# Two transformer layers on one core: router logits computed transposed, slot counts made by products, and the join of the layers filled with more shared-expert tiles

## The chip, the cores and the metric

The kernel runs on one core of one Trainium2 chip. A core has a matrix engine (TensorE, PE in the profile, its weight loads PEld), a vector engine (VectorE, DVE), an activation engine (ScalarE, ACT), a general engine (GpSimd, POOL) and a queue that only issues transfers (SyncE, SP). Each engine takes its instructions strictly in the order in which the program lists them for it; an instruction that waits holds up everything behind it on the same engine. The metric is the device time of one launch in microseconds (us); lower is better.

## The reference

Activations x have the shape 4 batches x 512 tokens x 256 features, all in float32. Two layers are applied, each with a modulated layer norm before an attention part and before a feed-forward part:

```python
h = layernorm(x) * (1 + ca) + sa;  x = x + ga * attention(h)
h = layernorm(x) * (1 + cb) + sb;  x = x + gb * ffn(h)
```

The six modulation vectors of a layer come from `silu(c) @ wmod`. In layer 0 the attention is linear (one key-value sum per feature), and the feed-forward part is a mixture of experts: a router with 32 experts in 8 groups (the best 3 groups are kept, softmax, best 6 experts), at most 48 token slots per expert over all batches, filled in the order of the tokens, so that they fill up early; and two shared experts for every token:

```python
logits = x @ gate_w.T                      # tokens x 32
pos  = cumsum(one_hot(flat_e)) - 1         # place of a pair in its expert
buf  = zeros(E * C + 1, h).at[slot].set(x[tok_idx])
out  = sum_k topk_w * expert(buf)[slot] + silu(x @ ws_g) * (x @ ws_u) @ ws_down
```

In layer 1 the attention is causal softmax attention (16 heads of 128), and the feed-forward part is a gated one whose three weights are made by cubic interpolation from control points.

## The kernel before

The work is staged in time like this; the stages overlap only at their edges.

**Front (0 to 148 us).** Modulation vectors, layer norm, linear attention, second norm and routing of the four batches. `choose(b)` (L546) makes the router logits: for each of the four 128-token tiles and each half of the features, a product with the 128x128 block of normalized activations as stationary operand and the 32 columns of the router weights as moving operand (L551). Each such product stands in the trace as two matmul records. Then some thirty small DVE instructions pick groups and experts; the 0/1 choices of a batch are `selb`, and a running sum of all earlier choices, `carry`, is made on DVE (L613, L615). `place(b)` (L617) turns choices into slot numbers by products on PE: a triangular matrix times `selb`, `ones` times the `carry` (L624), and `ones` times the earlier tiles of the batch (L628); then DVE compares the slot numbers with all the 48 slots (`oh`, L659), PE counts tokens from that (`pix`, L663). The shared experts' first products (`shared`, L706, tiles `sg` and `su`) have no one waiting for them and fill PE.

**Experts (148 to 230 us).** Sixteen pairs of experts. The order of PE is written out by hand in the loop at L960; the other engines' order is made by a planner that follows an estimate of each instruction's cost, except where `tc.issue_after(ins)` puts a block's instructions behind `ins` on that instruction's engine. For a pair q: the rows are fetched by an indirect transfer (`fetched`, `xg`, 8 buffers), turned (`turned`), multiplied with the pair's weights (`gate_up`), activated (ACT L822, DVE L823), turned again (`act_turned`), multiplied down (`down`), scaled into `ysb` (ACT L851, 4 buffers for the first 12 pairs) and written to two tables in memory, `ytab` by SP (L882) and `planes` by POOL's scatter (L867). Weights lie in 8 slots and are loaded as slots come free. Sixteen tiles of the shared experts' second product (`shared_down`, L724, tile `pd`, evicted by ACT at L735) are spread over the stage: four ahead of the loop, one in each of the iterations 0 to 5 (L967), two and four after the loop (L992, L994, L1002). The weights of layer 1's first three heads are loaded behind the last expert weights (L974), and ACT multiplies the three query weights by a constant (`scale_q`, L770, called at L1010).

**Join (about 216 to 245 us).** The twelve scattered pairs are read back from `planes` (`yr`, L921, 4 x 768 KB), summed and gated on DVE and POOL (`gated`, L932), the last four pairs are added through products (`combined`, `pcs`, `add_transposed`), which finishes x of batch 0. Then `norm(0)` of layer 1: statistics on DVE (L192, L193), a power on POOL (L196), normalization on DVE and ACT (L208, L212), eight turns on PE (L226, tile `lt_a`), eviction by ACT (L228) and DVE (L232), and the first projections (`project_first`).

**Heads (245 to 985 us) and feed-forward of layer 1 (985 to 1164 us).** 64 batch-head units. PE's order is written by hand (L1519 on). Between them run, on DVE, ACT and POOL, the interpolation of the weights (`spline`), the combination of its parts (`ffn_forms`, POOL, L1061) after units 1, 4 and 7, the gathers of expert results for batches 1 to 3 (POOL, L281), and the norm of the next batch. `ffn_norm(0)` is called at head 59 (L1586) for the first feed-forward batch.

## Time and profile before

| | us |
|---|---|
| three timed runs | 1163.98, 1165.59, 1167.76 (median 1165.59) |
| the profiled execution | 1165.69, span of its instructions 1164.0 |
| PE busy (share of the span) | 1118.4 (96%) |
| DVE, POOL, ACT busy | 850.9, 621.0, 541.5 |
| front, until the first `pd` product | 148.3 |
| experts, from there to the end of the last shared tile | 148.3 to 235.4 |
| turns of norm(0) of layer 1 | from 238.4 |

The profile gives each engine's busy time, the groups of instructions by source line, who waited for whom, and a timeline. In a row of the timeline the first number is the start in us from the first instruction, the second the length of the merged run, then engine, line, operation, written and read tiles, shapes, and in square brackets the idle time of that engine before the row and what ended it. PE and PEld rows overlap. A busy PE is not one at its peak: a matmul's record is longer than the time it takes from the next. The clock column says what share of its clock PE was granted in a stretch.

### The profile page before, as it was taken

The page shows a single profiled execution, that of the slowest core. Times are in us where ns is not written, and L with a number is a line of the kernel's source. Part 1 is how long each engine was busy: PE and PEld are TensorE (multiplying, and loading weights), DVE is VectorE, ACT ScalarE, POOL GpSimd, SP SyncE. Part 2 cuts the span into 40 slices and gives each one's busy share as a digit, 9 for nine tenths or more (in the row PEclk, how much of TensorE's full clock was granted, in tenths as well). Part 3 has the DMA queues.
Part 4 walks back from the last instruction along what each step waited for, and adds up shares of the span by engine and source line. Part 5 has one row for each costly group of instructions (what it writes and reads, how often), then busy time and mean ns, then how long its engine had stood idle before and what let it go on. Part 6 is the DMA issues. An engine that isn't in the chain of part 4 may idle for free.

```text
span 1164.0 us, 16910 instructions
## 1 busy us (share of the span) xinstructions
PE 1118.4 (96%) x5231; PEld 822.6 (71%) x5231; DVE 850.9 (73%) x2573; ACT 541.5 (47%) x1380; POOL 621.0 (53%) x944
## 2 busy tenths in 40 slices
PE   7888999989999999999999999999999999999998
PEld 2444364557777777777777777777787777888887
DVE  5687534567878887888887887988877777566765
ACT  3652223345555555555555465555555455333321
POOL 4363224248874857864656975444635655344331
PEclk9998999899999999999999999999999999999999
DMA  7921379734411322520321431012010000000001
GB/s 264 289 68 46 98 238 287 223 101 95 77 46 53 67 68 38 91 68 28 78 40 43 95 64 60 28 37 69 19 46 19 25 13 1 1 1 19 19 1 36
DMA packets 80485, 86.09 MB, mean 74 GB/s; under 512 B 12158, under 2 KB 64748, under 8 KB 80268
## 3 DMA queue, kind: packets, MB, share of 16 engines
q1 hardware_dynamic: 67868, 70.19, 19.3%
q0 software_dynamic: 11712, 13.25, 7.2%
q10 hardware_dynamic: 816, 1.58, 0.4%
q8 instruction: 42, 0.69, 0.2%
q14 instruction: 47, 0.39, 0.1%
HBM read 73.84 MB, written 11.55 MB: 73 GB/s over the span
## 4 chain that ended last, share of the span: by engine, by line
PE 72%; DVE 8%; POOL 4%; ACT 3%; issue 2%; DMA 2%; SPq 0%; ACTq 0%; POOLq 0%; DVEq 0%
PE s L1308 10%; PE o L1349 10%; PE po L1044 7%; PE P0p L1044 6%; PE fP L1044 6%; PE pt L1340 5%; PE P1p L1044 4%; PE P2p L1044 4%; PE acc L1044 3%; PE P0v L1044 3%; PE P2v L1044 2%; PE P1v L1044 2%; POOL ysum L281 1%; PE gu L814 1%; PE sg L713 1%
## 5 line engine op out<-in xcount | busy, mean ns | idle before, releaser
L1323 ACT ACTIVATE p<-s,nm 128x512 f32<-128x512 f32 (+3 forms) x256 | 135.4, 529 | 117.2 <-DVE nm L1320 114.7
L1308 PE MATMUL s<-qk,qk 128*128 128x512 f32 (+3 forms) x512 | 170.1, 434 | 1.1 <-DVE qk L1216 1.0
L1349 PE MATMUL o<-pT,v 128*128 128x512 f32 (+3 forms) x512 | 148.8, 433 | 0.3 <-DVE u3v L1228 0.3
L1349 PEld LDWEIGHTS o<-pT,v 128*128 128x128 f32 x512 | 96.8, 190 | 55.4 <-issue 30.6
L1342 ACT COPY pT<-pt 128x512 f32<-128x512 f32 (+1 forms) x192 | 98.5, 513 | 68.2 <-PE pt L1340 66.5
L1320 DVE TENSOR_REDUCE nm<-s 128x1 f32<-128x512 f32 (+3 forms) x256 | 124.0, 484 | 4.0
L281 POOL DMA_INDIRECT ysum<-ytab,code x72 | 113.6, 1578 | 20.4 <-issue 15.2
L1325 DVE TENSOR_SCALAR p<-p,den 128x512 f32<-128x512 f32 (+3 forms) x256 | 116.9, 457 | 3.4
L1340 PEld LDWEIGHTS pt<-ident,p 128*128 128x128 f32 x640 | 81.6, 141 | 34.5 <-issue 10.5
L1340 PE MATMUL pt<-ident,p 128*128 128x128 f32 x640 | 101.7, 273 | 0.3 <-DVE p L1325 0.3
L1318 DVE TENSOR_TENSOR s<-s,mask 128x128 f32<-128x128 f32 x256 | 73.5, 287 | 32.3 <-PE s L1308 32.3
L1183 POOL TENSOR_TENSOR w_p<-w_q,w_k 128x128 f32<-128x128 f32 x63 | 38.9, 617 | 84.3 <-ACT t1p L1222 51.9
L1308 PEld LDWEIGHTS s<-qk,qk 128*128 128x128 f32 x512 | 77.5, 191 | 5.5 <-issue 1.1
L1044 PE MATMUL P0p<-hT_a,w_q 128*128 128x256 f32 x252 | 75.0, 379 | 0.0
L1191 POOL TENSOR_TENSOR w_p<-w_k 128x128 f32<-128x128 f32 x63 | 29.9, 475 | 81.3 <-PE P2p L1044 81.3
L1044 PEld LDWEIGHTS P0p<-hT_a,w_q 128*128 128x128 f32 x252 | 47.5, 190 | 33.1 <-issue 29.9
L1324 DVE RECIPROCAL den<-den 128x1 f32<-128x1 f32 x256 | 40.4, 158 | 38.5 <-ACT p L1323 34.4
L1044 PE MATMUL P1p<-fT,w_p 128*128 128x256 f32 x252 | 65.0, 380 | 2.4 <-POOL w_p L1185 1.3
L1360 ACT ACTIVATE oH<-o,bia 128x512 f32<-128x512 f32 x64 | 44.0, 687 | 42.7 <-PE o L1349 41.5
L1216 DVE SCALAR_TENSOR_TENSOR qk<-P0p,bia,u3p 128x256 f32<-128x256 f32 x63 | 30.4, 482 | 37.4 <-ACT qk L1237 36.2
L1052 POOL TENSOR_TENSOR fI<-it 128x256 f32<-128x256 f32 x30 | 21.8, 728 | 67.0 <-DVE it L1641 67.0
L1044 PEld LDWEIGHTS P1p<-fT,w_p 128*128 128x128 f32 x252 | 47.6, 190 | 10.1 <-issue 2.2
(336 smaller groups left out, 2676.9 us busy)
## 6 DMA issues: line engine op xcount, KB each, us to landing
wg<-in_w_gate_up SPq DMA_DIRECT2D x16, 704.0 KB
w_q<-in_w_q SPq DMA_DIRECT2D x64, 128.0 KB
w_k<-in_w_k SPq DMA_DIRECT2D x64, 128.0 KB
w_v<-in_w_v SPq DMA_DIRECT2D x16, 512.0 KB
wd<-in_w_down SPq DMA_DIRECT2D x16, 352.0 KB
basis<-in_basis SPq DMA_DIRECT2D x8, 640.0 KB
planes<-zero SPq DMA_DIRECT2D x4, 768.0 KB
yr<-planes SPq DMA_DIRECT2D x4, 768.0 KB
```

What stands on the lines that cost most here:

```text
L281: ga = nc.gpsimd.indirect_dma_start(out=ysum[b][:, i, :], out_offset=None, in_=ytab[:, :], in_offset=bass.IndirectOffsetOnAxis(ap=code[:, ...
L1044: nc.tensor.matmul(out, lhsT=lhsT, rhs=rhs, start=start, stop=stop, skip_group_check=shared)
L1308: nc.tensor.matmul(s[:, at[i] : c], lhsT=qk[n, 0][:, i * P : (i + 1) * P], rhs=qk[n, 1][:, : (i + 1) * P], start=True, stop=True,)
L1318: nc.vector.tensor_tensor(s[:, e - P : e], s[:, e - P : e], mask, ALU.add)
L1320: nc.vector.tensor_reduce(nm, s[:, e - w : e], AX.X, ALU.max, negate=True)
L1323: nc.scalar.activation(p, s[:, e - w : e], AF.Exp, bias=nm, accum_out=den)
L1324: nc.vector.reciprocal(den, den)
L1325: nc.vector.tensor_scalar_mul(p, p, den)
L1340: nc.tensor.transpose(pt[:, c : c + P], probs[n, i][:, j * P : (j + 1) * P], ident)
L1342: nc.scalar.copy(pT, pt[:, :w])
L1349: nc.tensor.matmul(o[:, j * P :], lhsT=vs[n // 4][:, j, hc : hc + HD], rhs=pTs[n, j], start=(j == 0), stop=(j == NTT - 1),)
L1360: nc.scalar.activation(oT, o, AF.Identity, bias=bia[:, 2, h : h + 1])
```

## The change

Four things change.

1. **Router.** The logits are made transposed: the 32 router columns are the stationary operand, 128 tokens the moving one, and the four token tiles go to four 32-column groups, so that one 128x128 tile `pl` comes out. ACT copies it to memory on the chip (`lgT`), and PE turns it into the former layout. `carry` is gone; `place(b)` multiplies `ones` with every tile of every earlier batch instead (4, 8 and 12 products for batches 1 to 3), for which `selb` has four buffers.
2. **Shared tiles.** The iterations 3 to 5 of the loop lose their shared tile. After the loop there are two, then six, then, behind the eight turns of norm(0), one more.
3. **Join.** norm(0) is called inside the expert stage, with its tile in a freed weight slot, and PSUM buffers of that stage; the turned activations lie in a pool that is open earlier. The three `scale_q` stand behind the eviction of the first of the six tiles. `xg` has 7 buffers and is fetched 7 pairs ahead.
4. **Heads.** The first three `ffn_forms` are called at heads 8, 15 and 24 (so far 8, 14 and 20) and stand behind a named POOL instruction; the statistics of `ffn_norm(0)` stand behind the last DVE eviction of head 59's projection.

```diff
+NTAIL = 7
-        return pool.tile([P, 2, T], F32, tag="hT", name=f"hT_{name}{b}")
+        return pool.tile([P, 2, T], F32, tag="hT", name=f"hT_{name}{b}", bufs=B if name[1] == "0" else 2)
...
+        class Freed:
+            def tile(self, shape, dtype, tag, name, bufs=None):
+                return freed(self.tag, self.pair, shape, name)
...
-            lgv = ps.tile([P, NTT, E], F32, tag="tr", name=f"plg{b}")
-            for i in range(NTT):
-                for k in range(2):
+            pl = ps.tile([P, P], F32, tag="tr", name=f"plg{b}")
+            for k in range(2):
+                for i in range(NTT):
                     nc.tensor.matmul(
-                        lgv[:, i, :],
-                        lhsT=hTs[b][:, k, i * P : (i + 1) * P],
-                        rhs=gwT[:, k, :],
+                        pl[32 * i : 32 * i + 32, :],
+                        lhsT=gwT[:, k, :],
+                        rhs=hTs[b][:, k, i * P : (i + 1) * P],
                         start=(k == 0),
                         stop=(k == 1),
                     )
+            lgT = rp.tile([P, P], F32, tag="lgT", name=f"lgT{b}", bufs=1)
+            nc.scalar.copy(lgT, pl)
+            lgv = ps.tile([P, NTT, E], F32, tag="tr", name=f"plv{b}")
+            nc.tensor.transpose(lgv.rearrange("p i e -> p (i e)"), lgT, ident)
...
-            if b + 1 < B:
-                c = carry[b + 1] = rp.tile([P, 1, E], BF16, tag="carry", name=f"carry{b}")
-                parts = [selb[:, i, :] for i in range(NTT)] + ([carry[b][:, 0, :]] if b else [])
-                nc.vector.tensor_tensor(c[:, 0, :], parts[0], parts[1], ALU.add)
-                for x in parts[2:]:
-                    nc.vector.tensor_tensor(c[:, 0, :], c[:, 0, :], x, ALU.add)
...
-            if b:
-                nc.tensor.matmul(
-                    pos, lhsT=ones, rhs=carry[b].to_broadcast([P, NTT, E]), start=False, stop=False
-                )
+            for c in range(b):
+                for i in range(NTT):
+                    nc.tensor.matmul(
+                        pos,
+                        lhsT=ones,
+                        rhs=chosen[c][0][:, i : i + 1, :].to_broadcast([P, NTT, E]),
+                        start=False,
+                        stop=False,
+                    )
...
-                if q + 8 < NPAIR:
-                    fetched(q + 8)
+                if q + 7 < NPAIR:
+                    fetched(q + 7)
...
-                    if q < NI - NEXP - 6:
+                    if q < NI - NEXP - NTAIL - 2:
                         shared_down(NEXP + q)
...
-                shared_down(NI - 6)
+                shared_down(NI - NTAIL - 2)
                 combined(NPAIR - 1)
-                shared_down(NI - 5)
+                shared_down(NI - NTAIL - 1)
...
-                for i in range(NI - 4, NI):
-                    last_down = shared_down(i)
+                for i in range(NI - NTAIL, NI - 1):
+                    pd_copy = shared_down(i)
+                    if i == NI - NTAIL:
+                        with tc.issue_after(pd_copy.ins):
+                            for n in range(3):
+                                scale_q(n)
+                    if i == NI - 3:
+                        before_norm = pd_copy
+                hTs1[0] = new_hT(w4, 0, "a1")
+                ln_transposed(
+                    Freed("wg", NPAIR - NLOAD + NTT), ps, "gu", 1, 0, SA, CA, hTs1[0], "a1", None, None, before_norm
+                )
+                with tc.issue_after(last_pow[0].ins):
+                    shared_down(NI - 1)
...
-        for n in range(3):
-            scale_q(n)
...
-        ffn_h[b] = new_hT(hp, b, "f1"), normalized(np_, b, "f1", None, after, after)
+        ffn_h[b] = new_hT(w4s[0], b, "f1"), normalized(np_, b, "f1", None, after, after)
...
+        EARLY_FORMS = (8, 15, 24)
...
-                if unit in (1, 4, 7):
-                    ffn_forms(unit // 3, early[:, unit // 3])
...
+            if n in EARLY_FORMS:
+                with tc.issue_after(last_form[0].ins):
+                    ffn_forms(EARLY_FORMS.index(n), early[:, EARLY_FORMS.index(n)])
...
-                ffn_norm(0)
+                ffn_norm(0, evicted[n])
```

## The prediction

> **What bounds the kernel now.** I read the busy shares first, then PE's waits, then the timeline around each wait, and last the stretches with their granted clock. The page says that PE is the bound; so a change is worth what it does to PE's idle time, to its slowed stretches, and to its work where it never waits.

> ```profile
> PE 1118.4 (96%) x5231; PEld 822.6 (71%) x5231; DVE 850.9 (73%) x2573; ACT 541.5 (47%) x1380; POOL 621.0 (53%) x944
> PE 72%; DVE 8%; POOL 4%; ACT 3%; issue 2%; DMA 2%; SPq 0%; ACTq 0%; POOLq 0%; DVEq 0%
> ```

> The wait table of PE names four places that the change touches:

> ```profile
> PE gu L814 <- DVE xT L807: 4.1, 1, 4.1
> PE lt_a L226 <- ACT xn_a L208: 3.0, 1, 3.0
> PE pix L663 <- DVE oh L659: 3.5, 2, 2.0
> PE P1p L1044 <- POOL w_p L1185: 1.3, 1, 1.3
> ```

> The first looks like a wait for DVE; the timeline follows it back. ACT stands in `scale_q(0)`, which waits 5.22 us for layer 1's query weights; behind it stands the activation of pair 12, behind that DVE, behind that PE:

> ```profile
> 204.85 0.42 ACT L770 ACTIVATE w_q<-w_q 128x256 f32<-128x256 f32 x1 [5.22 <-DMA w_q<-in_w_q]
> 205.29 0.32 ACT L822 ACTIVATE act<-gu 128x176 f32<-128x176 f32 x1
> 205.64 0.34 DVE L823 TENSOR_TENSOR act<-act,gu 128x176 f32<-128x176 f32 x1 [4.53 <-ACT act L822]
> 206.37 2.61 PE L814 MATMUL gu<-wg,xT 128*64 128x352 f32 x8 [4.07 <-DVE xT L807]
> ...
> 211.42 1.35 PE L814 MATMUL gu<-wg,xT 128*64 128x352 f32 x8
> ...
> 212.86 1.02 POOL L867 DMA_INDIRECT planes<-ysb,didx  x1 [4.19 <-ACT ysb L851]
> ...
> 216.77 2.06 SPq L921 DMA_DIRECT2D yr<-planes  x4
> ...
> 223.14 0.96 DVE L937 TENSOR_TENSOR yr<-yr 128x768 f32<-128x768 f32 x1 [3.10 <-DMA yr<-planes]
> ...
> 235.88 1.05 POOL L196 TENSOR_TENSOR rs_a<-rs_a,nhalf 128x4 f32<-128x4 f32 x1 [8.59 <-DVE rs_a L195]
> ...
> 238.40 2.13 PE L226 MATMUL lt_a<-ident,xn_a 128*128 128x128 f32 x8 [2.96 <-ACT xn_a L208]
> ```

> The first `gu` after the gap takes 2.61 us where the next takes 1.35: the rows by stretch show why. Their last three figures are the clock granted to PE, the DMA share and GB/s; the clock is 0.73, 0.74 and 0.72 here and 1.00 in the stretches beside them.

> ```profile
> 202.00:207.00 5.00, 0.93 (x6) 0.45 (x7) 1.28 (x8) 1.57 (x5) 0.28 (x1) 0.73 0.69 219
> 207.00:215.00 8.00, 8.00 (x46) 3.92 (x44) 4.03 (x20) 2.92 (x8) 2.31 (x4) 0.74 0.41 73
> 236.00:242.00 6.00, 3.59 (x10) 2.24 (x11) 3.35 (x6) 1.87 (x3) 5.43 (x9) 0.72 0.32 115
> ```

> The reader sees a chain: last scatter 212.86, read-back 216.77, DVE without a pause from 223.14 to 235.8, PE's turns 238.40. PE is ahead of it by 2.96 us, so what counts for the join is when the last scatter leaves.

> **Expert stage.** (a) `scale_q` moves behind the first of six shared tiles. Gone are 4.07 us of gap and the slow iteration: `gu` to `gu` is 5.05 us (206.37 to 211.42) against 2.83 for the next (to 214.25), so 2.22; sum 6.29. Moved past: ACT alone. There the three (1.26 us) now precede the copies of the later shared tiles; two PSUM buffers cover it, and if not, 1.26. (b) Three shared tiles leave iterations 3 to 5: 4.12 us per iteration (167.13 to 171.25) falls to 2.84 (179.50 to 182.34), 3 x 1.28 = 3.84. Together the loop could be 10.1 us earlier. (c) What is late next: the four `ysb` buffers. `ysb` of pair 11 needs the `ytab` write of pair 7 landed; that was issued at 191.55 and landed at 204.45 (landing events), and the DMA share is 0.87 to 1.05 from 150 to 202, so fewer PE instructions don't bring it forward. Pair 11's `ysb` stood at 211.64; without this limit it would be at 201.5, with it at about 204.5: I take 204.5, since DMA is full: 7.1 earlier, 10.1 as the bound. (d) Then the scatter 1.22 later (211.64 to 212.86) and its landing: 3.73 us for this one, 6.16 for the one at 198.41 with weights in flight; at 205.7 the last of them still land (208.2), so 4.9, and 0.2 to the read-back: 210.8 against 216.77, **6.0 earlier**. (e) `xg` with 7 buffers: a fetch leaves in iteration q+1 and is needed in q+5, 4 x 2.84 = 11.4 us less some 3.3 for `ysb`, scatter and issue; landings took 7.0 to 7.3. Nothing, with a margin of 0.8; if gone, up to 0.5 per pair on eight pairs, of which the limit in (c) hides 3. (f) PE before the turns: earlier by 7.9 (pair 12's `y` starts at 205.45 instead of 213.33), plus two tiles of 1.29 (24 matmuls in 5.36): 235.43 becomes 230.1, still ahead of the turns at 232.4, so those two cost nothing; if the loop were not earlier they would cost what exceeds 2.96. (g) The last tile behind the turns: 1.29, between turns that end at 240.5 and a second half of `hT` that DVE delivers at 241.43; the first products lay in there. Between 0.4 and 1.3, I take 0.9, because those products fill the hole already. (h) `w_o` and `basis` on SP may start some 10 us later, behind the freed slots; `w_o` landed at 237.0 and is first read at 276.9, `basis` at 239.4 and 308.6. Nothing. Sum: -6.0 + 0.9 = **-5.1** (bounds -9.2 with neither limit of (c) nor (d), -1 if `ytab` lands 2 later and a scatter takes 6.2 plus a wait in (e)).

> **Front.** Here the planner makes a new order, so this is the least certain part. Rows:

> ```profile
> 87.57 1.34 DVE L615 TENSOR_TENSOR carry<-carry,selb 128x32 bf16<-128x32 bf16 x2
> ...
> 90.95 0.35 PE L663 MATMUL pix<-oh,tok 128*32 128x384 bf16 x4 [1.97 <-DVE oh L659]
> ...
> 112.69 1.64 PE L551 MATMUL plg<-gwT,hT_m 128*128 128x32 f32 x14
> ...
> 101.39 0.59 ACT L721 ACTIVATE sT<-sg 96x512 f32<-96x512 f32 x1 [12.14 <-PE sg L713]
> ```

> Logits: 16 matmul records a batch at 0.106 us (1.48 between first and last of 14) are 1.7. The new ones stream 128 float columns, 0.107 each by the eight turns `at_d` (1.04 with 0.2 of latency): 1.7 if they go one by one, 0.4 if four column groups overlap as `pix` does (four of 384 columns in 0.35, eight in 0.51, so 0.16 for four). `pix` is the nearest; with the turn 0.25, a batch saves 1.0, bounds +0.3 and -1.1. Only where PE doesn't wait does it count: batch 3 whole (PE has 3.6 us of gaps between 108 and 148), the others by a third: -2.0. Counts: 24 products for 3, at 0.055 (starts of `pos`), 21 x 0.055 = 1.2, of it 0.6 in batch 3, and 0.3 of the rest: +0.9. DVE loses eleven adds, 3.4 us; in batch 1 they take 2.3 (0.69, 1.34, 0.28) just ahead of `posb` and `oh`, on which PE waits 1.97: -2.0. ACT copy and turn add 0.8 of latency a batch (0.37 as in L735, 0.27, two hand-overs). At the end that is covered: rows of pair 0 landed at 138.4 and are turned at 150.67. But PE stands at the turn if the planner leaves nothing in between; 0 to 3.2, and behind a waiting ACT up to 12.1 (last row). I take 1.0. `selb` with four buffers, `lgT` and the moved `hT` add no instruction: nothing. Sum **-2.1**, bounds -6.5 (the stretch at half clock from 91.7 to 98.5, 0.66 over 90 to 100, goes too, 3.4, with the further -1.0 of the copy) and +13.

> The trace has 32-column products among 128-column ones at `pix`: the next `sg` starts at 128.36, before the records of `pix` end (128.08 and 0.35), so no pause shows. [...]

> **Heads.** POOL's `ffn_forms(2)` at 495.3 stands behind four gathers and ahead of the weight forms for which PE waits 1.27 (the P1p row above); at head 24 no gathers stand: -1.27. `ffn_norm(0)` was run by DVE at 764.7 to 767.9, and PE waited 1.86 for a value eviction behind it (769.23); it moves to head 59, where DVE is busy 15.9 of 25: -1.86. There its chain (statistics 2.2, power 1.05, normalization 1.4) has one unit of 10.7 us before PE's turns: 0, or up to 3 if DVE puts it last; I add 0.6. The forms at heads 8 and 15 stay where POOL has no queue: nothing, or the 1.1 that POOL stood idle before those of 415.8. Sum **-2.5**, bounds -3.1 and +2.

> **Sum.** -5.1 - 2.1 - 2.5 = -9.7. The profiled execution took 1165.69 (span 1164.0, 1.7 around it), 0.1 above the median 1165.59: **1156.0**.

> The rows show 0.74 after the gap of 4.07 and 0.72 after that of 2.96, so the sum leaves the join's slowed products as they are behind its remaining gap of 2.3. [...]

> **Rivals.** *R1, the front gives its gain back*: copy and turn cost 1.8 a batch, 7.1, not 1.0: 1156 + 6.1 = 1162.1. For it: two PSUM buffers `tr` are now held at once by a batch's logits, and the next batch's turns use them. Against: PE has shared products in reserve until 148. *R2, transfers keep the expert stage where it is* (bounds of (c), (d), (e)): -1 instead of -5.1, 1160. For it: the DMA shares; against: expert weights land 11.7 us or more before use (pair 15's at 202.55, read at 214.25). *R3, slower*: at PE's new turn of `lgT`, TensorE stands in order behind ACT. One batch behind the 12.1 wait, with a half-clock stretch (3.4) after it, so 15.5 for the 1.0 in the sum: 1156 + 14.5 = 1170.5. It decides once the four turns together cost over 14.1 (1169.1 less 1156, and the 1.0). For: ACT idles 12.14 and 5.82 us behind `sg` in batches 2 and 3. Against: the copy needs only `pl`, which in batch 2 would be ready ahead of that `sg`. *R4, more*: no half-clock stretch at 92 (3.4), DMA no limit (4.1): 1148.5.

> **How the numbers follow.** 0.3% (3.5 us) is about what a measurement of this kernel can tell from no change: 1162.1 and 1169.1 are the lines. Chances: forecast 0.50 (own range 1152 to 1160), R1 0.16, R2 0.13, R3 0.13, R4 0.08. Faster: 0.50 + 0.13 + 0.08 + half of R1 0.08 = 0.79; same: the other half and a little of R3, 0.10; slower 0.11. The range leaves out R3 and the far half of R4, 0.17: 1149.5 to 1166.

> **What will show it.** Right: no ACT wait for `w_q` in the loop; read-back near 209 (front included); the first `gu` of pair 13 at about 1.35; turns of norm(0) near 230; no `plg` row over 0.6; no PE wait of over 1 us at 498 and 767. Wrong: PE idle before the turn of `lgT`; `ysb` waiting for `ytab` past 206; DVE late for head 59's `lt_f`. A new order by the planner in stages that the change doesn't touch would move the time without any of this.

## The result

The changed kernel took 1154.18 us in the median of six runs (1152.02 to 1155.01), the kernel before 1165.72 beside it: a ratio of 0.9894, 95% interval 0.9873 to 0.9915, or 11.5 us less. The forecast was 1156.0. The profiled execution took 1152.55, 1.6 below its median; its span is 1150.7 against 1164.0, so the two traces differ by 13.3, 1.8 more than the medians.

Two lines of the changed kernel's page, busy time and the chain that ended last by engine:

```profile
PE 1112.7 (97%) x5256; PEld 816.5 (71%) x5256; DVE 848.0 (74%) x2562; ACT 541.2 (47%) x1384; POOL 622.8 (54%) x944
...
PE 75%; DVE 9%; ACT 3%; issue 2%; POOL 2%; DMA 1%; SPq 0%; ACTq 0%; DVEq 0%; POOLq 0%
```

PE is still the bound. Where the 13.3 went, by marks that both traces have:

| stretch | before | after | difference | forecast |
|---|---|---|---|---|
| start to the first shared `pd` product | 148.28 | 145.41 | -2.9 | -2.1 |
| from there to the turns of norm(0) | 90.12 | 80.95 | -9.2 | |
| turns to the first scores product `s` | 7.60 | 8.07 | +0.5 | -5.1 for both |
| first scores product to the end | 918.0 | 916.3 | -1.7 | -2.5 |

PE's waits in the changed kernel (total, times, longest):

```profile
PE lt_m L227 <- DVE xn_m L213: 6.4, 4, 3.5
...
PE pix L676 <- DVE oh L672: 3.0, 4, 1.8
...
PE gu L827 <- DVE act L836: 1.3, 2, 0.8
...
PE pj L1067 <- ACT ysum L748: 0.5, 1, 0.5
```

The 4.07 ahead of `gu` and the 2.96 ahead of `lt_a` are gone, and so are the waits of 1.27 and 1.86 in the heads. New are 0.78 and 0.51 ahead of two early `gu`, and 0.46 ahead of `pj`. The end of the expert stage and the join, by the timeline:

```profile
198.40 0.32 ACT L835 ACTIVATE act<-gu 128x176 f32<-128x176 f32 x1 [0.78 <-issue]
...
199.83 1.40 PE L827 MATMUL gu<-wg,xT 128*64 128x352 f32 x8
...
200.04 0.95 ACT L864 ACTIVATE ysb<-y,xg 64x256 f32<-64x256 f32 x2 [1.33 <-PE y L850]
...
201.27 1.02 POOL L880 DMA_INDIRECT planes<-ysb,didx  x1 [1.75 <-DMA ytab<-ysb]
...
205.57 2.10 SPq L934 DMA_DIRECT2D yr<-planes  x4
...
220.31 1.03 ACT L783 ACTIVATE w_q<-w_q 128x256 f32<-128x256 f32 x3
...
225.81 0.73 DVE L213 TENSOR_SCALAR xn_a<-x,ag_a,rs_a 128x256 f32<-128x256 f32 x2
...
226.36 1.47 PE L227 MATMUL lt_a<-ident,xn_a 128*128 128x128 f32 x8
...
227.67 1.46 PE L741 MATMUL pd<-wsd,sT 128*128 128x256 f32 x6
...
229.60 1.98 PE L1067 MATMUL pj<-hT_a,w_q 128*128 128x512 f32 x4 [0.46 <-ACT ysum L748]
```

Every `gu` takes 1.40, pair 11's `ysb` (200.04) waits for PE alone, `scale_q` stands at 220.31 and finds its weights there, and the turns start without a wait, 0.55 after DVE began on their rows: PE and DVE arrive together. The same end in stretches (PE, PEld, DVE, ACT, POOL busy, granted clock, DMA share, GB/s):

```profile
192.00:197.00 5.00, 5.00 (x34) 2.10 (x31) 1.29 (x5) 2.06 (x5) 1.08 (x2) 1.00 0.90 296
197.00:205.00 8.00, 8.00 (x57) 4.04 (x58) 4.69 (x24) 3.44 (x9) 2.60 (x4) 1.00 0.75 220
226.00:234.00 8.00, 7.49 (x30) 4.38 (x29) 4.36 (x8) 3.34 (x7) 5.16 (x8) 1.00 0.29 100
```

The clock is 1.00 in all three, where the kernel before had 0.72 to 0.74.

### The profile page after: what moved, and what is told of

Its sections match the earlier page's. It is cut to its first block, busy times and chain, and to the rows that moved or that the text cites. A ratio compares the mean times of both kernels' runs of the same rounds, so it can differ in the third digit from the quotient of the medians.

```text
span 1150.7 us, 16944 instructions
## 1 busy us (share of the span) xinstructions
PE 1112.7 (97%) x5256; PEld 816.5 (71%) x5256; DVE 848.0 (74%) x2562; ACT 541.2 (47%) x1384; POOL 622.8 (54%) x944
## 4 chain that ended last, share of the span: by engine, by line
PE 75%; DVE 9%; ACT 3%; issue 2%; POOL 2%; DMA 1%; SPq 0%; ACTq 0%; DVEq 0%; POOLq 0%
PE s L1330 11%; PE o L1371 10%; PE po L1067 8%; PE P0p L1067 7%; PE fP L1067 6%; PE pt L1362 6%; PE P1p L1067 4%; PE P2p L1067 4%; PE P0v L1067 3%; PE acc L1067 3%; PE P2v L1067 2%; PE P1v L1067 2%; PE gu L827 2%; PE y L850 1%; DMA w_q<-in_w_q 1%
## 5 line engine op out<-in xcount | busy, mean ns | idle before, releaser
L1362 PEld LDWEIGHTS pt<-ident,p 128*128 128x128 f32 x640 | 81.7, 141 | 34.2 <-issue 10.7
L1205 POOL TENSOR_TENSOR w_p<-w_q,w_k 128x128 f32<-128x128 f32 x63 | 39.5, 626 | 82.3 <-ACT t1p L1244 54.9
```

Source lines behind the costliest of these rows:

```text
L1362: nc.tensor.transpose(pt[:, c : c + P], probs[n, i][:, j * P : (j + 1) * P], ident)
```

## The experiments

Theory and rivals: the gain is mostly the expert stage (`scale_q`, three tiles), then the front, then the heads, and each term can be undone by itself. Against it stand transfers that hide the expert stage's part, and a front whose gain is not the router's. After the first four runs a theory on the clock (G) and one on the `ytab` writes (D) joined. Two marks are used below: **E**, from the first `pd` product to the turns of norm(0) (90.12 before, 80.95 after), and **F**, from the turns `lt_m` of batch 1 to the first `pd` product (86.06 before, 83.12 after). F leaves out the logits of batch 0, which come ahead of it; from the turns of batch 0 (at 43.29 and 43.93) to `pd` it is 104.99 and 101.48. What lies ahead of those differs between executions: by the table of run 5 they start at 42.69 to 43.96.

**1. `scale_q` alone, in the kernel before.**

```diff
                 for i in range(NI - 4, NI):
                     last_down = shared_down(i)
+                    if i == NI - 4:
+                        with tc.issue_after(last_down.ins):
+                            for n in range(3):
+                                scale_q(n)
...
-        for n in range(3):
-            scale_q(n)
```

> The kernel before, with one part of the change alone: the three scalings of the query weights stand behind the first of its four last shared tiles. Theory A (the prediction's step (a)): the gap of 4.07 ahead of gu of pair 13 and the slow iteration behind it (2.22) go; ysb of pair 11 then stands at 211.64 - 6.29 = 205.4, just behind the landing of pair 7's ytab write (204.45), so that limit takes nothing; scatter and landing give back 0.8 (3.73 to some 4.5), the turns of norm(0) come 5.5 earlier: 1160.2. Rival B (the ACT wait only covered something else that is late, an expert weight or xg): at most 2 earlier, 1163.7, and a new wait shows ahead of one of the last gu.

1159.28 in the median, ratio 0.9956 (0.9935 to 0.9978). E is 83.63, 6.5 less than before, with no wait left ahead of a `gu`: theory A, a little more than it said. But 3.39 of idle time, with two slowed cells behind it (a cell is a stretch of 3.41 us; slowed, its clock is 0.50; see the last section), now stood ahead of the turns, so that to the first scores product only 5.3 of it was left; by the medians the edit is worth 5.4 (1164.63 beside it). Unexpected was the front, which this kernel doesn't touch: the first `pd` product stood at 144.93, not 148.28. See 4 and 5.

**2. The same wait put back into the changed kernel.**

```diff
+                scaled = scale_q(0) if q == 12 else None
+                with after_or_not(scaled):
-                nc.scalar.activation(act[q], gu[:, 0:INT], AF.Silu)
+                    nc.scalar.activation(act[q], gu[:, 0:INT], AF.Silu)
```

> The changed kernel, with the first scaling put back ahead of pair 12's activation, where the kernel before had it. By the changed kernel's trace the first query weights land at 198.42 and that activation stood at 195.03. Theory A: ACT waits 3.4, the activation stands at 198.85, gu of pair 13 starts some 1.1 behind it, at 199.9 instead of 196.94; a gap of 3.0 on PE brings the half clock (as 2.96 did at the join before), some 2.0 more; PE's turns had no wait, so all of it shows: +5.0, 1159.2. Rival B: with the three shared tiles out of the loop the wait is covered: PE waits under 1, +0.5, 1154.7. Rival C: a gap of 3.0 leaves the clock alone: +3.0, 1157.2.

1158.58, ratio 0.9947 (0.9929 to 0.9966); E is 87.15, 6.2 more than in the first trace of the changed kernel and 4.8 more than in its second (82.31, run 4). From its timeline:

```profile
200.40 0.42 ACT L783 ACTIVATE w_q<-w_q 128x256 f32<-128x256 f32 x1 [4.82 <-DMA w_q<-in_w_q]
...
200.84 0.53 ACT L837 ACTIVATE act<-gu 128x176 f32<-128x176 f32 x2
...
201.67 0.64 PE L843 MATMUL act_t<-ident,act 128*88 128x128 f32 x2 [5.37 <-DVE act L838]
```

ACT waits for the query weights, one activation stands behind it, and PE stands behind that for 5.37 (more than the 3.0 expected, because the weights landed at 200.4, against 198.4 in the first trace). Theory A; rival B is out. Runs 1 and 2 price the wait from both kernels: 6.5, and 4.8 to 6.2, where step (a) said 6.3.

**3. The three tiles back in the loop.**

```diff
-NTAIL = 7
+NTAIL = 4
```

> The changed kernel with four shared tiles behind the experts, as before, not seven: three tiles are back in iterations 3 to 5. Theory A: last scatter and read-back come 3 x 1.28 = 3.84 later, so normalized rows stand at 229.8 instead of 226.0; PE has 3.9 less to do ahead of the turns, so it waits there for some 3.6, at half clock behind it for 3.4 (1.2 lost): +4.8, 1159.0. Rival B (the prediction's limit (c): the transfers set the end of the loop, so the tiles were covered): the last scatter stays within 1 of 201.3, +0.5, 1154.7.

1155.14, ratio 0.9930 (0.9905 to 0.9955). In the profiled execution E is 84.23, 3.3 more than in the first trace of the changed kernel, and to the first scores product 4.6 more, near theory A's 4.8. The end of its chain, by the timeline:

```profile
202.94 1.02 POOL L880 DMA_INDIRECT planes<-ysb,didx  x1 [1.76 <-ACT ysb L864]
...
207.08 2.12 SPq L934 DMA_DIRECT2D yr<-planes  x4
...
229.55 2.04 PE L227 MATMUL lt_a<-ident,xn_a 128*128 128x128 f32 x8 [5.29 <-DVE xn_a L213]
```

But not in theory A's way. Part of it is the read-back's second block, which took 7.5 to land, against 5.9 in the first trace; and PE, 5.29 early, lost a slowed cell. What the tiles do in the loop shows from the first `pd` product to `ysb` of pairs 7 and 11, in the traces that have `scale_q` moved and no other edit in the loop (run 8, with one more tile ahead of the turns, is left out):

| tiles | trace | `ysb` 7 | `ysb` 11 | E |
|---|---|---|---|---|
| in the loop | run 1 | 40.08 | 56.38 | 83.63 |
| in the loop | this run | 40.09 | 56.38 | 84.23 |
| behind it | changed kernel, first trace | 40.16 | 54.63 | 80.95 |
| behind it | changed kernel again (run 4) | 36.57 | 56.08 | 82.31 |
| behind it | `a_router_old` | 36.56 | 57.62 | 84.84 |
| behind it | `a_logits_old` | 36.56 | 55.83 | 83.05 |
| behind it | `a_counts_old` | 36.56 | 56.72 | 83.93 |
| behind it | `a_heads_old` | 36.76 | 55.60 | 81.44 |

Up to pair 7 the loop without the tiles is 3.3 to 3.5 earlier in five of six traces, nearly the 3.84 of step (b). At pair 11 it is between 0.8 earlier and 1.2 later: ACT had waited for `ytab` writes in between (run 4), so limit (c) took the gain back. In the first trace the loop was late by pair 7 (waits of 0.78 and 0.51 for DVE; what caused them is open), then waited for no write and ended 1.8 earlier. So the 3.3 in E holds for the best of six traces, and rival B has the end of the loop right in most. By the medians the tiles are worth 1.0 to 2.4 (1155.14 against 1154.18 and 1152.70); the profiled execution, 2.4 above its own median, shows more than that.

**4. The router of before, and the changed kernel again.** The first is the diff's hunks in `choose` and `place` taken back, the second is the changed kernel as it is.

> The changed kernel with the router of before: logits by 128x32 products, untransposed, and the counts carried over by adds on DVE. The first shared down product stood at 148.28 before and at 145.41 in the changed kernel. Theory A: all of the front's 2.87 is the router: it stands at 148.3 again, the half-clock stretch behind 91 is back at 6.8 long, 1157.1. Theory A2 (the prediction's sum of the terms): +2.1, 1156.3. Rival B: a part comes from something else in the front (the order of the planner, moved hT): under +1, 1155.

> The changed kernel once more, beside the next three and with more executions. Theory G (the clock grant is decided on a grid of 3.41: every slowed stretch of the traces so far starts a whole number of 3.413 behind the others of its trace, and follows a grid cell in which PE stood 1.97 or more; the grid's phase differs from execution to execution): the shared down products start at 145.1 to 145.5 again, with one or two slowed cells just behind the gap of 3.46 ahead of the turns at 85.8; the cell that is slowed lies at another place by up to 3.41. Theory D (transfers): pair 11's ysb stands at 200.0 where the ytab writes take some 11, and up to 3 later where they take 14 or more. 1154.2 in all. Rival: phase and transfers are the same in every execution, and all marks repeat within 0.2.

`a_router_old`: 1155.94, ratio 0.9935 (0.9909 to 0.9961), first `pd` at 148.82, F 86.00. `after_again`: 1152.70, ratio 0.9885 (0.9865 to 0.9906), first `pd` at 144.32, F 83.28. So the router's front is 2.9 longer in one execution, as theory A says, and yet run 1, with the same router, had F 83.02. That execution of `a_router_old` was a long one, 1160.78; by the medians its router costs 1.8 to 3.2. The clock tells the two fronts apart. Stretches of the kernel before, with the columns of the last such rows:

```profile
88.00:92.00 4.00, 2.03 (x16) 1.48 (x14) 3.93 (x8) 0.60 (x1) 1.74 (x4) 0.96 0.48 155
92.00:98.00 6.00, 6.00 (x22) 2.82 (x21) 2.60 (x7) 0.00 (x0) 0.00 (x0) 0.50 0.00 1
```

The same of run 1:

```profile
84.00:88.00 4.00, 4.00 (x16) 2.46 (x15) 3.90 (x13) 2.87 (x4) 3.83 (x7) 0.57 0.08 20
88.00:98.00 10.00, 9.28 (x52) 4.68 (x50) 8.59 (x28) 0.60 (x1) 1.53 (x3) 1.00 0.17 58
```

Before, PE's wait of 1.97 ahead of `pix` is followed by 6.8 at half clock (from 91.7), with DVE busy for 2.60 of six us and ACT not at all: F is 3.0 longer than in run 1. There one slowed cell lay earlier, from 84.2 to 87.6, and PE came late enough that only 0.72 of the wait was left. What the clock records of all fourteen traces have in common stands in the section on the hardware below.

`after_again` also shows theory D. ACT and PE in its last iterations:

```profile
195.42 0.95 ACT L864 ACTIVATE ysb<-y,xg 64x256 f32<-64x256 f32 x2 [2.93 <-DMA ytab<-ysb]
...
200.40 0.95 ACT L864 ACTIVATE ysb<-y,xg 64x256 f32<-64x256 f32 x2 [3.69 <-DMA ytab<-ysb]
...
201.40 1.08 PE L850 MATMUL y<-wd,actT 88*64 88x256 f32 x8 [1.90 <-ACT ysb L864]
```

Pair 11's `ysb` waits for pair 7's `ytab` write, as step (c) had it, and PE for the `ysb` ahead of pair 12's `y` (the expectations call it pair 11's). The three writes that were waited for took 13.1 to 14.4 here, from their issue to the `ysb`; pair 7's took about 11.3 in the first trace. A wait of PE of that kind, 1.7 to 2.3 long, is there in six traces (`a_router_old`, `after_again`, `a_heads_old`, `a_logits_old`, `a_counts_old`, `a_last_ahead`). The rival (marks repeat within 0.2) is out for E: 80.95 and 82.31 for the same kernel. A difference of less than 1.4 in E between two single traces therefore shows nothing by itself.

**5. The router in halves.** `a_logits_old` has the logits of before with the changed counts, `a_counts_old` the changed logits with the counts of before.

```diff
-            lgT = rp.tile([P, P], F32, tag="lgT", name=f"lgT{b}", bufs=1)
-            nc.scalar.copy(lgT, pl)
-            nc.tensor.transpose(lgv.rearrange("p i e -> p (i e)"), lgT, ident)
+                        lgv[:, i, :],
+                        lhsT=hTs[b][:, k, i * P : (i + 1) * P],
+                        rhs=gwT[:, k, :],
```

> The changed kernel with the untransposed 128x32 logit products of before (16 a batch, no copy, no turn), the counts as changed. Start of the shared down products, 145.4 in the changed kernel: theory A (the prediction's terms: 2.0 of PE time less 1.0 for copy and turn): 146.4, 1155.2. Theory G (the front's gain is the clock's: no slowed cells behind 91): where no cell is slowed 144.9 to 145.4, and 148.3 where two are; 1154.2 or 1157.5. Rival: copy and turn cost more than the products save: 144.4, 1153.2.

```diff
-            for c in range(b):
-                for i in range(NTT):
+            if b:
-                        rhs=chosen[c][0][:, i : i + 1, :].to_broadcast([P, NTT, E]),
+                    pos, lhsT=ones, rhs=carry[b].to_broadcast([P, NTT, E]), start=False, stop=False
```

> The changed kernel with the counts carried over by adds on DVE as before, the logits as changed (transposed and turned). Theory A (the prediction's terms: 2.0 of DVE adds back, 0.9 of products gone): the shared down products at 146.5, 1155.3, the gap ahead of batch 1's pix back at 2 us (0.62 now). Theory G: that gap of 2 alone, if it falls into one grid cell, slows the next one or two: 148.5, 1157.3; if the grid splits it, 145.5. Rival: the carry adds lay beside other work, 144.5, 1153.3.

| logits | counts | first `pd` | from batch 0's turns | F | PE busy, idle until `pd` | median |
|---|---|---|---|---|---|---|
| before | before (run 1) | 144.93 | 101.94 | 83.02 | 122.7, 22.2 | |
| before | changed | 142.00 | 99.30 | 80.38 | 123.6, 18.4 | 1150.57 |
| changed | before | 146.69 | 102.73 | 84.38 | 121.2, 25.4 | 1156.03 |
| changed | changed (first trace) | 145.41 | 101.48 | 83.12 | 122.1, 23.3 | 1154.18 |
| changed | changed (`after_again`) | 144.32 | 101.63 | 83.28 | 122.1, 22.2 | 1152.70 |

The medians stand at ratios of 0.9863 (0.9836 to 0.9889) for the first and 0.9913 (0.9888 to 0.9938) for the second. The counts are the gain: some 0.9 more PE work (busy time, with what slowed cells add to it), 2.2 to 3.8 less waiting. The transposed logits, with the order that the planner makes around them, are a loss: 1.5 less PE work, 3.2 to 4.9 more waiting, so that from batch 0's turns to `pd` it takes 2.2 to 2.3 longer (0.8 with the counts of before). This is the rival of the first expectation, and a miss for theory A on the logits; theory G's 144.9 is missed too, since the counts gain without the clock. PE's waits in the front say where (up to 146 us). First `a_logits_old`:

```profile
PE lt_m L227 <- DVE xn_m L213: 5.8, 4, 3.9
...
PE pos L626 <- DVE selb L617: 1.0, 1, 1.0
...
PE pix L672 <- DVE oh L668: 0.6, 1, 0.6
...
PE sg L722 <- ACT sT L730: 0.3, 1, 0.3
```

Then the changed kernel:

```profile
PE pix L676 <- DVE oh L672: 3.0, 4, 1.8
PE su L726 <- DVE sT L735: 1.6, 1, 1.6
PE sg L726 <- ACT sT L734: 1.4, 2, 0.7
```

Of the 4.9 between these two traces `pix` has 2.4, the shared tiles `su` and `sg`, which wait for evictions, 2.7, `lt_m` 0.6, and `pos` gives 0.8 back. The longest wait for `oh`, with batch 1's logits in between, in the changed kernel's timeline:

```profile
65.40 0.22 PE L630 MATMUL pos<-selb,tri 128*128 128x128 bf16 x1
...
65.63 0.65 PE L562 MATMUL plg<-hT_m,gwT 128*32 128x128 f32 x16
65.74 0.29 DVE L650 TENSOR_SCALAR posb<-pos 128x128 bf16<-128x128 f32 x1
...
66.34 0.27 ACT L570 COPY lgT<-plg 128x128 f32<-128x128 f32 x1 [0.21 <-PE plg L562]
...
67.17 0.27 PE L572 MATMUL plv<-ident,lgT 128*128 128x128 f32 x1
...
67.60 0.27 DVE L530 TENSOR_SCALAR kv<-kv,n 128x1 f32<-128x1 f32 x1 [1.57 <-POOL n L529]
67.79 3.21 DVE L672 TENSOR_TENSOR oh<-posb,iota_c 128x1536 bf16<-128x1536 bf16 x3
...
69.22 0.35 PE L676 MATMUL pix<-oh,tok 128*32 128x384 bf16 x4 [1.78 <-DVE oh L672]
```

`pos` and `pix` are batch 0's. Its slot numbers lie ready at 66.03; then DVE stands for 1.57 at `kv`, a piece of the linear attention that waits for POOL, and `oh` and PE stand behind it. The logits have no part in this wait.

The sixteen products take 0.65, as step "Logits" had it (0.4 and the turn), and the logits are readable 1.8 behind the first product; untransposed, batch 0's sixteen take 1.87. So copy and turn use up what the products save, and PE never stands at the turn itself (the wait that rival R3 feared). But their latency doesn't explain the loss either: batch 0's logits can be read 9.0 behind its turns in both kernels, and the last `pix` starts 85.3 behind them, in `a_logits_old` 86.5. What is left is the new order of PE, DVE and ACT around these instructions. No run holds that order fixed, so this part is argued, not shown.

**6. The heads as before.**

```diff
-            if n in EARLY_FORMS:
-                with tc.issue_after(last_form[0].ins):
-                    ffn_forms(EARLY_FORMS.index(n), early[:, EARLY_FORMS.index(n)])
+                if unit in (1, 4, 7):
+                    ffn_forms(unit // 3, early[:, unit // 3])
...
-                ffn_norm(0, evicted[n])
+                ffn_norm(0)
```

> The changed kernel with the three edits in the heads undone (the forms of the next layer's weights behind units 1, 4 and 7 of the spline, the normalization of batch 0 not held behind head 59's eviction). Theory A (the prediction's sum of -2.5): from the first scores product to the end 916.3 becomes 918.8, +2.5, 1156.7, with PE's waits of 1.27 and 1.86 back. Theory A' (by the two traces, 918.0 to 916.3): +1.7, 1155.9. Rival B (the waits only move to other heads): within 0.5.

1155.43, ratio 0.9917 (0.9896 to 0.9937), 2.7 above `after_again` beside it and 1.3 above the first measurement. From the first scores product to the end it takes 919.1, against 916.3 and 916.8. Its waits:

```profile
PE P2v L1067 <- DVE v L1237: 2.5, 4, 1.9
...
PE P1p L1067 <- POOL w_p L1207: 1.0, 1, 1.0
```

Both are back (1.86 and 1.05), and the 1.86, which here fell into one clock cell, has a slowed one behind it (757.4 to 760.9). Rival B is out by these waits. Theory A and A' can't be told apart: the eleven traces with the changed heads took 916.1 to 918.4 (median 916.8), the other two with those of before 917.6 and 918.0.

**7. The `ytab` writes on ACT's queue.**

```diff
-                nc.sync.dma_start(out=ytab[1 + q * P : 1 + (q + 1) * P, :], in_=ysb)
+                nc.scalar.dma_start(out=ytab[1 + q * P : 1 + (q + 1) * P, :], in_=ysb)
```

> The changed kernel with the ytab writes issued on ACT's queue, directly behind the ysb that they read, not on SP's behind the loads of the next expert weights. Theory D (the prediction's limit (c) is there, but it is the place in SP's queue, not a ceiling of the transfers): the landing of those writes falls from 11 to 15.5 to the 6 to 7 that the scatters of the same ysb take on POOL's queue; no ysb waits for ytab, and PE's wait of 1.9 ahead of y of pair 11 (seen in three of four traces of the changed kernel's expert stage) is gone; the turns of norm(0), 80.95 to 82.3 behind the first shared down product, come at about 80.5; 1151.5. Rival (the sixteen engines are full, any queue waits alike): latencies of 11 and more stay, the wait stays, and ACT's sixteen issues of 0.43 cost up to 1: 1153.5.

1155.25, ratio 0.9924 (0.9899 to 0.9948), E 84.35. Theory D holds in its mechanism: the writes of pairs 0 to 8, of which those waited for had taken 13.1 to 15.1 on SP's queue (six traces), land in 5.7 to 7.9, and no `ysb` waits for one. A new wait ate the gain:

```profile
188.54 0.33 ACTq L895 DMA_DIRECT2D ytab<-ysb  x1
...
196.66 0.33 ACTq L895 DMA_DIRECT2D ytab<-ysb  x1
...
197.08 0.32 ACT L835 ACTIVATE act<-gu 128x176 f32<-128x176 f32 x1 [5.03 <-DMA wg<-in_w_gate_up]
...
198.16 2.28 PE L827 MATMUL gu<-wg,xT 128*64 128x352 f32 x8 [3.38 <-DVE xT L820]
```

One of the sixteen issues stood on ACT until 196.66, just behind the landing of pair 15's weights (issued at 180.89, 15.69 later), and held the activation behind it, as `scale_q` had. That issue has no need of those weights. But the trace has both transfers reporting on one semaphore (106), and at 196.60, just ahead of the issue, an instruction of ACT that waits for it.

**8. The last tile ahead of the turns.**

```diff
-                for i in range(NI - NTAIL, NI - 1):
+                for i in range(NI - NTAIL, NI):
...
-                with tc.issue_after(last_pow[0].ins):
-                    shared_down(NI - 1)
```

> The changed kernel with the last shared tile ahead of the turns of norm(0), as before, not behind them. Theory A (the prediction's step (g): behind the turns it costs 0.9): from the turns to the first scores product 8.07 becomes 7.2, but the turns move 1.3 later where PE is the bound there: +0.4 in all, 1153.2. Theory B (by the changed kernel's trace, where pj waits 0.46 for that tile's copy on ACT): the tile fills the time in which hT is evicted; ahead of the turns PE waits for hT about as long: +0.9, 1153.6. Rival (the wait of pj for the copy goes and nothing takes its place): -0.5, 1152.2.

1154.49, ratio 0.9910 (0.9878 to 0.9941). From the turns to the first scores product it takes 6.84, 1.2 less than with the tile behind them:

```profile
228.92 1.04 PE L227 MATMUL lt_a<-ident,xn_a 128*128 128x128 f32 x8
...
230.95 1.95 PE L1064 MATMUL pj<-hT_a,w_q 128*128 128x512 f32 x4 [0.99 <-DVE hT_a L233]
```

So behind the turns the tile fills a hole of 0.99, and yet the stretch is 1.2 longer: the tile takes 1.29, the turns 0.43 more (1.47 against 1.04), and `pj` waits 0.46 for the tile's copy. Whether the move pays as a whole stays open: this trace also has the 2.26 wait for `ysb` and a slowed cell ahead of the turns, and its interval covers both theories.

**9. Two versions meant to beat both.** `best` is `a_logits_old` with the `ytab` writes of run 7. `best2` is `a_logits_old` with

```diff
+                if q in (10, 11):
+                    ysb = freed("wg", q, [P, D], f"ysb{q}")
+                else:
...
```

> The changed kernel with two edits: the untransposed logits of before (2.1 faster by its own run), and the ytab writes on ACT's queue. Theory D: the wait of 2.15 ahead of y of pair 11 and the slowed cell behind it (1.7) go too; the two add up, but by then DVE's chain ahead of the turns (0.3 behind PE) takes the place of PE: -2.1 - 2.5 = 1148.1. Rival (DVE's chain was the bound at the join already): 1150.5, as with the logits alone.

> The changed kernel with two edits: the untransposed logits of before, and ysb of pairs 10 and 11 in the freed weight slots of their own pairs, so that they wait for no ytab write; no queue's order changes. Theory D (the reuse of the four ysb buffers is the limit (c), and the wait of 2.15 ahead of y of pair 11 is all that it costs): that wait and the slowed cell behind it go; the turns of norm(0) come 80.4 to 81.0 behind the first shared down product (83.05 with the logits alone), PE waits there for DVE up to 0.5; 1150.6 - 2.0 = 1148.5. Rival (something else is as late: an expert weight, xg, or DVE's chain ahead of the turns): a new wait in the last iterations or above 1.5 ahead of the turns, 1150.5.

`best`: 1153.93, ratio 0.9912 (0.9887 to 0.9937); run 7's wait is in it (3.83 ahead of a `gu`, E 84.87), which neither theory had. `best2`: 1150.23, ratio 0.9876 (0.9851 to 0.9901), E 81.00 against 83.05 with the logits alone, no wait ahead of `y` and none at the turns. The marks go as theory D says, but the changed kernel's first trace had E 80.95 and no wait for a write without this edit, and the time does not confirm it: 1150.23 and 1150.57 are the same here. Both lie below the changed kernel's 1152.70 and 1154.18, and the intervals of the ratios overlap with its own: some 2 us better is likely, not settled.

## Why the prediction was right, and where it was not

The time fell into the forecast's own range (1152 to 1160), 1.8 below the number. By steps:

- **(a) `scale_q`, 6.29: right.** 6.5 by run 1, 4.8 to 6.2 by run 2.
- **(b) three tiles, 3.84: right in the loop, and taken back by (c).** 3.3 to 3.5 at pair 7 in five of six traces, -1.2 to 0.8 of it left at pair 11. The first trace came to 1.8 at pair 11 in another way (run 3). The prediction had the two together at 7.1 and not 10.1, which is this limit.
- **(c) the `ytab` limit: right mechanism, about the right size, wrong reason.** `ysb` of pair 11 was put 56.2 behind the first `pd`; in the six traces that waited it stood at 55.6 to 57.6, in the first trace at 54.6, where it waited for nothing. The reason given was that a full set of DMA engines can't be brought forward. The DMA share was 0.96 before and 0.99 after in the twenty us from 20 behind the first `pd`, but with 278 and 311 GB/s: a share near 1.00 was no ceiling on bytes. Run 7 shows what it is instead: the place of the write behind weight loads in SP's queue (13.1 to 15.1 where it was waited for; 5.7 to 7.9 on ACT's).
- **(d), (f): mis-sized in the first trace, nearer in the second.** The read-back was issued 60.2 behind the first `pd` against 68.5 before: 8.3 earlier, not 6.0 (6.8 in `after_again`). The turns followed at -9.2 (-7.8). PE's predicted 2.3 of idle time ahead of them was none (0.41 in `after_again`), and with it the slowed products went, which the sum had kept: the clock from 226 to 234 was 1.00, where it was 0.72 from 236 to 242 before.
- **(g) last tile, 0.9:** 1.2 by run 8, inside its bounds.
- **(e), (h): right.** PE waits for no `xg`, `w_o` or `basis` in the changed kernel.
- **Front, -2.1: nearly right as a sum, by errors that cancel, so by luck.** Counts: +0.9 and -2.0 in the text, +0.9 and -2.2 to -3.3 with the changed logits (run 5). Logits: -2.0 in the text, -1.5 of PE work. Copy and turn: +1.0 in the text, 3.2 to 4.9 of waiting with the transposed logits in the runs. This is the step that failed. Rival R1 named the place, at 7.1 and for another reason; the runs show the loss, and that it isn't the latency, but not which part of the new order makes it. The clock hid it: in two of three traces with the router of before the stretch at half clock behind the wait of 1.97 made the front 3 longer (F 86.06 and 86.00 against 83.02). Where it did not (run 1), it is 101.94 from batch 0's turns to `pd`, against 101.48 and 101.63: the change gains under 0.5 in the front.
- **Heads, -2.5:** -1.7 by the two traces; both waits are gone, and by run 6 come back with 2.3 to 2.8, a slowed cell of up to 1.7 included.
- **Rivals.** R2 is out as a whole: from the first `pd` to the scores the two traces gained 8.7 and 7.3, not 1; but its condition is there, in the waits for `ytab`. R3 is out: no wait at any turn of `lgT`. R4's half is in the result: its slowed stretch at 92 gave way to one cell at 86.

The sum of 9.7 against 13.3 in the traces (11.5 in the medians) leaves out 3.6. By the cells at half clock, the pair at 92 and the one at 238 are gone beyond what the sum has and one at 86 is new, 3.4 + 1.7 - 1.7 = 3.4: the clock can be most of it. That is a sum over one pair of traces; no run holds the clock alone.

What the prediction read at `pix`, 32-column products among 128-column ones without a pause, holds for the new logits: batch 1's sixteen (from 65.63, 0.65 together) start before the `pos` ahead of them ends (65.70), and the next product starts at 66.20, before they end (66.28), so no pause shows.

## What to carry to other kernels

An instruction that waited for a transfer no one needed yet held up what stood behind it on its engine (6.5 by run 1): move it behind the point where its data has surely landed, and look through the queue that it is moved into in the same way (run 7). Less work on PE is not yet less time: the transposed logits saved 1.5 of work, and 3.2 to 4.9 of waiting came with them, so count PE's idle time up to a mark, not its busy time. When a gain is taken out of a loop, ask what is late next: 3.5 at pair 7 was gone at pair 11. And before a gain in one stage is credited to an edit, compare the clock cells there: the same front differed by 3 us in two executions.

## What the hardware showed that was not expected

| PE idle in a cell of 3.41 | next cell full | next cell half |
|---|---|---|
| 1.97 or more | 0 | 27 |
| 1.70 to 1.97 | 6 | 4 |
| 1.20 to 1.70 | 43 | 1 |
| under 1.20 | 4513 | 0 |

So in these traces a gap of some 2 us cost up to 1.7 more for each slowed cell (half of 3.41) where it fell into one cell, and nothing where the grid left under 1.20 of it in each. Before, 1.97 at 88.98 to 90.95 lay within one cell, and the next two were slowed; of the 1.86 at 767.37 to 769.23 the grid left 1.73 in one, and the next was full. In a slowed cell less idle time went with a second one: with 0.55 to 1.01 the next cell was slowed again (five times), with 0.05 to 0.47 it wasn't (three times). A slowed cell with PE busy throughout was followed by a full one, except in the kernel before and `a_router_old` at 92, where the cell holds the untransposed 32-column products; whether these are the reason stays open.

The mean granted clock was 0.9911 over 58 executions of the kernel before and 0.9967 over twelve of the changed one: (0.9967 - 0.9911) x 1160 = 6.5 us of PE's clock, an estimate of the most that the clock can have of the 11.5, since PE can be idle in a slowed cell anyway (2.07 of the one at 204.30 before).
